# Row preparations due at the second place behind their turning, and k's turning behind its combining, in the second input stage of a transformer block

## The chip, the cores and the metric

The kernel runs on one core of a Trainium2 chip. Its engines work in parallel, each through its own queue in order: TensorE (PE, matrix products; PEld is its weight load), VectorE (DVE), ScalarE (ACT), GpSimd (POOL) and SyncE (SP, which here only starts DMA transfers). GpSimd and ScalarE start DMA transfers too. On-chip data lie in SBUF, and PE writes its sums to PSUM, eight banks of 128 partitions by 512 float32 numbers. The metric is the device time of one execution in microseconds (us).

## The reference

One block of a diffusion transformer with conditioning, in float32: batch B = 2, N = 2048 tokens, C = 576 features, H = 16 heads of 36, and an MLP of width 2304.

```python
mod = silu(c) @ w_ada + b_ada
sh_msa, sc_msa, g_msa, sh_mlp, sc_mlp, g_mlp = split(mod, 6)
xn = ln(x, 1e-6) * (1 + sc_msa) + sh_msa
q, k, v = split_heads(xn @ w_qkv + b_qkv)
q = ln(q, 1e-5, qn_g, qn_b); k = ln(k, 1e-5, kn_g, kn_b)
attn = softmax(q @ k.T * hd**-0.5)
x = x + g_msa * (attn @ v @ w_proj + b_proj)
xn2 = ln(x, 1e-6) * (1 + sc_mlp) + sh_mlp
x = x + g_mlp * (gelu(xn2 @ w1 + b1) @ w2 + b2)
```

What matters here is the third and fourth step for the second batch element: the products that give q, k and v, the norm of q and k over the 36 numbers of each head, and how their rows reach the layout in which the attention reads them.

## The kernel before

The program goes through these stages: the inputs of batch element 0 (`inputs` with b = 0), its attention (`attend`), its output projection (`outputs`), then the same three for element 1, and the MLP for both. The change touches only the input stage of element 1, `in_pairs` inside `inputs`, and of the later stages only the start of the second attention lies near it.

**Pairs of token tiles.** The 2048 tokens are 16 tiles of 128 (NT = 16). Tiles 0 and 1 are done one by one; then a loop takes pairs t0 = 2, 4, ..., 14. For each pair and for each of k (w = 1), q (w = 0) and v (w = 2), in this order, `seven_products` computes the 2 x 2 block product with seven block products instead of eight (sums of the inputs and of the weights are formed beforehand). PE writes them in four groups, (1), (2, 6), (5, 7) and (4, 3), each into one tile `s` of two PSUM banks. There are four such tiles, so group i of the next product needs the tile that group i of this one has filled.

**Combining.** `combined` gives the work that empties these tiles: ScalarE copies product 1 (`copied`), and five DVE steps, `do[0]` to `do[4]` (lines 1253 to 1257), make the outputs. `do[0]` reads (2, 6), `do[1]` reads (5, 7), `do[2]` product 4, `do[3]` product 5 and `do[4]` product 3. So (2, 6) is free behind `do[0]`, (5, 7) behind `do[3]`, (4, 3) behind `do[4]`. The prediction counts these as steps 1 to 5.

**Finishing.** `finishing` returns five pieces for k or q of a pair: the square on ScalarE (`ks`, `qs`), the sum over each head on DVE (`kr`, `qr`, L1296), the root on ScalarE (`kq`, `qq`), the reciprocal on DVE with the scaling on GpSimd (`kd`, `qd`, L1303 and L1305), and the turning, `turned_out` (`kt`, `qt`): DVE transposes 32 x 32 squares (L1309), and eight DMA transfers store the rows by feature in DRAM (L1312), seven from SP's queue and one from GpSimd's.

**Row preparations.** The attention reads keys and queries by feature from SBUF tiles `km`, `ke` (keys) and `qm`, `qe` (queries of one block of 512). For the first head pair their rows are fetched within this stage, as soon as they are stored: `turned_out` calls `take_k_block` or `take_q`, which issue the loads on SP (L817 and L819) and return the DVE work that follows, the row preparations. A key block has one preparation, with four DVE instructions (L852 on `km`; L852, L861 and L862 on `ke`). The queries have two: one instruction on `qm`, and three on `qe`. These are put into the list `taken`. Key tiles 0 to 3 are taken with k of pair 2, tiles 4 to 7 with pair 6, 8 to 11 with pair 10, 12 and 13 with pair 12, 14 and 15 with pair 14; the queries of tiles 0 to 3 with q of pair 2, whose turning stands in the loop's next round.

**The order.** The queues of DVE, SP, GpSimd and ScalarE run in the order in which the program is written here, and so does PE's. `rows_made` takes one entry of `taken`, if there is one, and issues its DVE work. It is called at three places of a round: behind `do[0]` of k, behind `do[1]` of q, and behind `qd` in v's part (this last not in the last pair). Behind v's `do[1]`, the rest of v's combining and q's turning are put off to the next round, where they stand behind ScalarE's copy and ahead of k's `do[0]`. What is left in `taken` at the end of the stage, one preparation, goes to the attention.

**The next pair's tokens.** Each round issues the loads of the next pair's tokens at its start on GpSimd's queue (`features_begun`); behind `kd`, ScalarE applies scale and shift (`input_modulated`), and GpSimd forms the sums for the seven products (`token_sums`).

Of the kernel before, what the change touches and what calls it, by code (L numbers as in the profile page):

```python
# [31 lines left out]
def dit_block(  # L32
# [724 lines left out]
    def block_of_small():  # L757
# [53 lines left out]
        def rows_taken(queue, main, ends, halves, first, src, dst):  # L811

            rest = HD - DIMS
            for c in halves:
                for h in range(2):
                    r0, f0 = 32 * (2 * c + h), first + h * HD
                    queue.dma_start(out=main[r0 : r0 + DIMS, dst], in_=qk_rows["dram"][f0 : f0 + DIMS, src(c)])  # L817
                    values = qk_rows["dram"][f0 + DIMS : f0 + HD, src(c)]
                    queue.dma_start(  # L819
                        out=ends[r0 : r0 + 4 * rest, dst],  # L820
                        in_=values.unsqueeze(1).to_broadcast([rest, 4, values.shape[1]]),
                    )
# [26 lines left out]
        def scaled(dst, part, rows, w, of_ends=0):  # L849

            gain, bias = (gb_at[rows, of_ends, i, w : w + 1] for i in range(2))
            nc.vector.tensor_scalar(dst, part, gain, bias, ALU.mult, ALU.add)  # L852
# [39 lines left out]
        def take_q(p, qb):  # L892
            i, full = qb % 2, slice(0, P)
            src = lambda c: slice(qb * BLK, (qb + 1) * BLK)
            rows_taken(nc.sync, qm[i], qe[i], range(2), p * 2 * HD, src, slice(0, BLK))
            return [lambda: scaled(qm[i], qm[i], full, 0), lambda: parted(qe[i], full, 0)]
# [190 lines left out]
        def inputs(b, weights, making, work, xnts, turned, loaded):  # L1087

            wq, wq4, bq = weights
            both, squares, taken = {}, {}, []  # L1090
# [166 lines left out]
                    lambda: tt(dst(0, 1), dst(0, 1), single(out[3]), ALU.add),  # L1257
                ], lambda: nc.scalar.copy(one, out[1])

            pairs = {}  # L1260

            def token_sums(t0):

# [9 lines left out]
            def features_begun(t):  # L1273
                if t < NT and t not in xnts:
                    xnts[t] = input_loaded(turned.pop(t), nc.gpsimd, work if t % 4 == 3 else None)

            def pair_opened(w, t0):
                pairs[w] = work.tile([P, 2, C], F32, name="pair", bufs=4)
                both.update({(w, t0 + t): pairs[w][:, t, :] for t in range(2)})

            def flat(w):
                return pairs[w].rearrange("p t f -> p (t f)")

            def finishing(w, t0):

                pair = flat(w)
                n = 2 * H
                held_ = {}

                def squares_made():  # L1290
                    held_["sq"] = work.tile([P, 2 * C], F32, name="sq", bufs=1)
                    nc.scalar.activation(held_["sq"], pair, AF.Square)

                def summed_up():
                    var = held_["var"] = work.tile([P, n], F32, name="var", bufs=2)
                    nc.vector.tensor_reduce(var, held_["sq"].rearrange("p (h d) -> p h d", d=HD), AX.X, ALU.add)  # L1296

                def rooted():
                    nc.scalar.activation(held_["var"], held_["var"], AF.Sqrt, bias=eps5, scale=1.0 / HD)

                def divided():
                    inv = work.tile([P, n], F32, name="inv", bufs=2)
                    nc.vector.reciprocal(inv, held_["var"])  # L1303
                    heads = pair.rearrange("p (h d) -> p h d", d=HD)
                    nc.gpsimd.tensor_tensor(heads, heads, inv.unsqueeze(2).to_broadcast([P, n, HD]), ALU.mult)  # L1305

                def turned_out():
                    turned_qk = work.tile([P, 2 * C], F32, name="turned_qk", bufs=2)
                    nc.vector.transpose(turned_qk, pair)  # L1309
                    for t in range(2):  # L1310
                        for g in range(P // SQ):
                            (nc.gpsimd if 2 * t + g == 5 else nc.sync).dma_start(  # L1312
                                out=by_square[t0 + t, g][:, w * NSQ : (w + 1) * NSQ, :],
                                in_=turned_qk[g * SQ : (g + 1) * SQ, t * C : (t + 1) * C].rearrange(
                                    "p (k j) -> p k j", j=SQ
                                ),
                            )
                    if w == 1:
                        if t0 % 4 == 2 and t0 < NT - 2:
                            taken.append(take_k_block(t0 - 2, t0 + 2))  # L1320
                        elif t0 >= NT - 4:
                            taken.append(take_k_block(t0, t0 + 2))
                    elif t0 == TPB - 2:
                        taken.extend(take_q(0, 0))

                return squares_made, summed_up, rooted, divided, turned_out

            def rows_made():
                if taken:
                    taken.pop(0)()  # L1330

            def in_pairs():

                sums = work.tile([P, 4, 2, 3, HALF], F32, name="weight_sums")
                less = work.tile([P, 3, HALF], F32R, name="wq4_less")
                nc.sync.dma_start(out=less.bitcast(F32), in_=saved["less"])
                for w in (1, 0, 2):
                    nc.sync.dma_start(out=sums[:, :, :, w, :], in_=saved["sums"][:, :, :, w, :])
                spread, ones = bias_rows()

                for w in (1, 0):
                    pair_opened(w, 0)
                features_begun(3)
                k = product(1, 0)
                biased(1, k, 0)
                q = product(0, 0)
                biased(0, q, 0)
                v = product(2, 0)
                biased(2, v, 0)
                k = product(1, 1)  # L1350
                biased(1, k, 1)
                input_modulated(b, xnts[3])
                more = token_sums(2)
                ks, kr, kq, kd, kt = finishing(1, 0)
                ks(), kr(), kq(), kd()
                q = product(0, 1)
                biased(0, q, 1)
                qs, qr, qq, qd, qt = finishing(0, 0)
                qs(), qr(), qq()
                kt()  # L1360
                qd()
                v = product(2, 1)
                biased(2, v, 1)
                rest = [qt]

                for t0 in range(2, NT, 2):
                    last = t0 == NT - 2
                    operands = sums, less, spread, ones, more
                    for t in range(2):
                        features_begun(t0 + 2 + t)  # L1370

                    pair_opened(1, t0)
                    do, copied = combined(1, t0, seven_products(1, t0, operands))
                    copied()
                    for step in rest:
                        step()
                    do[0]()
                    rows_made()
                    do[1]()
                    do[2](), do[3](), do[4]()  # L1380
                    ks, kr, kq, kd, kt = finishing(1, t0)
                    ks()

                    pair_opened(0, t0)
                    do, copied = combined(0, t0, seven_products(0, t0, operands))
                    copied()
                    kr(), kq()
                    do[0]()
                    kd()
                    if not last:  # L1390
                        for t in range(2):
                            input_modulated(b, xnts[t0 + 2 + t])
                        more = token_sums(t0 + 2)
                    do[1]()
                    rows_made()
                    kt()
                    do[2](), do[3](), do[4]()
                    qs, qr, qq, qd, qt = finishing(0, t0)
                    qs()

                    do, copied = combined(2, t0, seven_products(2, t0, operands))
                    copied()
                    qr(), qq()
                    do[0]()
                    qd()
                    if not last:
                        rows_made()
                    do[1]()
                    if not last:
                        rest = [*do[2:], qt]  # L1410
                        continue
                    do[2](), do[3](), do[4]()
                    qt()
                    return taken
# [89 lines left out]
            taken = key_rows[-2:]  # L1504
# [711 lines left out]
```

## Time and profile before

| | us |
|---|---|
| median of three runs | 3165.39 (3161.59 to 3166.11) |
| the profiled execution, as timed | 3166.04 |
| its span in the profile | 3164.7 |
| second input stage, first pair product to first score of the attention | 1111.85 to 1318.82 |
| attention behind it and the rest | 1318.82 to 3164.70 |

The profile is of one execution. A time such as 1141.03 counts from the span's start. In a row of a timeline stand the start, the duration, the engine, the source line, the operation, output and inputs by name, their shapes and the count; in brackets how long the engine had been idle before and what it waited for. In the view of waits, a row names who waited, for whom, how long in total, how many times, and the longest. In the table of windows, a row gives a stretch of time and its length, the busy time of each engine in it, the mean clock granted to PE (1.00 is full), the share in which the DMA engines were busy and GB/s.

### The profile page before, as it was taken

To read this page: it belongs to the slowest core of one execution; us is meant where nothing else is said; L and a number is where in the kernel's file an instruction comes from. 1 tells how busy PE (TensorE), PEld (TensorE's weight loads), DVE (VectorE), ACT (ScalarE), POOL (GpSimd) and SP (SyncE) were. 2 spreads that over 40 slices of the span, in tenths; PEclk is the share of its full clock that TensorE was granted. 3 is DMA by queue.
4 is the path that set the end of the run, shared out by engine and by line. 5 is a ranking of instruction groups with operands and counts; after the bars stand their busy time and mean duration, and the time that the engine had idled before them with its cause. 6 is when DMAs were issued, how large, how long until landed. Compare 5 with 4: busy or idle time off the path is not lost. (4 is left out here: it accounts for less than half of the span.)

```text
span 3164.7 us, 46996 instructions
## 1 busy us (share of the span) xinstructions
PE 3112.9 (98%) x17511; PEld 1856.2 (59%) x17511; DVE 1566.2 (49%) x2287; ACT 1477.3 (47%) x2853; POOL 713.5 (23%) x1005
## 2 busy tenths in 40 slices
PE   8999999999999988999999999999999999999999
PEld 5883333333334767633333333358888888777777
DVE  6773444444444555434443444345566554545454
ACT  2336666766666023366666666633565552000000
POOL 4550110123321444200011111012333320111121
PEclk9999999999999999999999999999999999999999
DMA  5773332233341743411122222145544444333331
GB/s 146 185 144 86 104 88 57 74 95 90 95 112 52 232 78 70 87 43 34 46 59 71 77 64 69 56 153 189 163 133 136 132 116 159 111 120 116 117 105 39
DMA packets 294838, 324.65 MB, mean 103 GB/s; under 512 B 168904, under 2 KB 225160, under 8 KB 292488
## 3 DMA queue, kind: packets, MB, share of 16 engines
q1 hardware_dynamic: 246464, 198.32, 21.8%
q0 software_dynamic: 46960, 117.92, 14.3%
q10 hardware_dynamic: 1176, 5.31, 0.5%
q8 instruction: 141, 2.31, 0.3%
q14 instruction: 97, 0.79, 0.1%
HBM read 200.50 MB, written 110.43 MB: 98 GB/s over the span
## 5 line engine op out<-in xcount | busy, mean ns | idle before, releaser
L1531 ACT ACTIVATE pt<-b 128x512 f32<-128x512 f32 x2048 | 1057.5, 610 | 482.9 <-PE b L1540 267.3
L1540 PE MATMUL b<-pt,vt 128*64 128x512 f32 x4096 | 935.0, 598 | 2.1 <-ACT pt L1531 2.1
L1540 PEld LDWEIGHTS b<-pt,vt 128*64 128x64 f32 x4096 | 271.8, 136 | 584.3 <-issue 437.7
L1527 PE MATMUL b<-qm,km 32*128 32x512 f32 x4096 | 563.8, 613 | 0.0
L1592 DVE TENSOR_TENSOR ot<-b,ot 128x512 f32<-128x512 f32 x192 | 132.8, 692 | 589.0 <-PE b L1540 589.0
L1527 PE MATMUL b<-qe,ke 16*128 16x512 f32 x2048 | 420.2, 791 | 0.0
L2128 PE MATMUL s<-ws,as 128*128 128x288 f32 x1440 | 351.8, 406 | 0.0
L1527 PEld LDWEIGHTS b<-qm,km 32*128 32x128 f32 x4096 | 190.6, 184 | 271.2 <-ACT pt L1531 211.1
L2128 PEld LDWEIGHTS s<-ws,as 128*128 128x128 f32 x1440 | 273.6, 190 | 75.6
L1143 PE MATMUL s<-wq,xnt 128*128 128x288 f32 x864 | 226.9, 406 | 2.6 <-ACT xnt L400 2.1
L1559 DVE RECIPROCAL den<-den 128x512 f32<-128x512 f32 x64 | 213.6, 3337 | 11.7 <-DMA den<-den_dram 11.7
L1968 PE MATMUL m<-xnt,wb 128*128 128x256 f32 x864 | 210.6, 379 | 2.7 <-DVE cs L2002 1.8
L1968 PE MATMUL m<-s,wb 128*128 128x256 f32 x864 | 210.0, 379 | 0.0
L1590 DVE COPY ot<-b 128x512 f32<-128x512 f32 x64 | 44.3, 692 | 275.0 <-PE b L1540 275.0
L1143 PEld LDWEIGHTS s<-wq,xnt 128*128 128x128 f32 x864 | 157.8, 190 | 38.3 <-ACT xnt L400 1.6
L1968 PEld LDWEIGHTS m<-s,wb 128*128 128x128 f32 x864 | 164.2, 190 | 22.3
L1527 PEld LDWEIGHTS b<-qe,ke 16*128 16x128 f32 x2048 | 106.7, 184 | 114.0 <-issue 113.3
L1968 PEld LDWEIGHTS m<-xnt,wb 128*128 128x128 f32 x864 | 158.8, 190 | 22.7 <-DVE cs L2002 2.4
L2006 ACT ACTIVATE cs<-cs,b_sb 128x512 f32<-128x512 f32 x144 | 98.9, 719 | 113.9 <-DVE cs L2001 90.2
L1047 POOL DMA_DIRECT2D turned<-squares x160 | 107.5, 679 | 196.1 <-DVE squares L1042 188.5
L1064 ACT ACTIVATE xnt<-xnt,mod 128x128 f32<-128x128 f32 x244 | 100.4, 481 | 102.0 <-DMA weight_sums<-sums_kept 51.5
L2128 PE MATMUL s<-ws,hidden 128*128 128x288 f32 x576 | 142.3, 406 | 0.0
(257 smaller groups left out, 3293.3 us busy)
## 6 DMA issues: line engine op xcount, KB each, us to landing
gelu<-cs SPq DMA_DIRECT2D x144, 256.0 KB
hidden<-gelu SPq DMA_DIRECT2D x16, 2304.0 KB
spare<-in_x_dram POOLq DMA_DIRECT2D x64, 288.0 KB, 3.2
x_dram<-spare POOLq DMA_DIRECT2D x64, 288.0 KB, 2.5
qm<-qk SPq DMA_DIRECT2D x256, 64.0 KB
den<-den_dram SPq DMA_DIRECT2D x128, 128.0 KB
xnt<-turned POOLq DMA_DIRECT2D x56, 256.0 KB, 4.0
turned<-squares POOLq DMA_DIRECT2D x160, 72.0 KB, 2.6
```

The lines of the kernel that those rows point to most:

```text
L1047: queue.dma_start(out=by_square[g], in_=squares[g * SQ : (g + 1) * SQ, :].rearrange("p (k j) -> p k j", j=SQ))
L1064: nc.scalar.activation(part, part, AF.Identity, **affine(which, k, b))
L1143: nc.tensor.matmul(out_a, full[:, k, :], wq[:, k, f], start=k == 0, stop=False)
L1527: nc.tensor.matmul(ps, k[r, keys], q[r, :], start=first, stop=not first)
L1531: nc.scalar.activation(pt[:, h, :], banks[2 * c + h], AF.Exp, scale=SCALE)
L1540: nc.tensor.matmul(acc[64 * h : 64 * h + 64, :], vt[:, v0 : v0 + 64], pt[:, h, :], start=pt is pts[0][0], stop=pt is pts[-1][0],)
L1559: nc.vector.reciprocal(den, den)
L1590: nc.vector.tensor_copy(ot, acc)
L1592: nc.vector.tensor_tensor(ot, acc, ot, ALU.add)
L1968: nc.tensor.matmul(out_m[m], wb[:, slot[m], k, f * P : (f + 1) * P], moving[m](k), start=k == 0 and m in (1, 2, 5, 6), stop=k == 1 and m == 1,
L2006: nc.scalar.activation(part, part, AF.Gelu, bias=b1_sb[:, g : g + 1])
L2128: nc.tensor.matmul(ms[m], stationary[m][:, f, :], ws[m][:, f, :], start=(f == 0), stop=(f == HF - 1))
```

## The change

The list `taken` gets a second list beside it, `slots["due"]`, with one number for each entry, and a counter `slots["now"]` that `rows_made` raises by one at each call. An entry is due two calls behind its turning, and `rows_made` does nothing while the first entry isn't due. The call of `rows_made` behind k's `do[0]` is taken out, so that a round has two places: behind `do[1]` of q, and behind `qd` in v's part.

k's turning, `kt`, stood between q's `do[1]` and `do[2]`. It now stands behind q's `do[4]`, except in the last pair (t0 = 14), where it stays, and where `rows_made` is called behind `do[4]` instead. The loads of the key rows are issued in `kt`, so they move with it.

```diff
-            pairs = {}
+            pairs, slots = {}, {"now": 0, "due": []}
...
+                    before = len(taken)
                     if w == 1:
                         if t0 % 4 == 2 and t0 < NT - 2:
                             taken.append(take_k_block(t0 - 2, t0 + 2))
...
                     elif t0 == TPB - 2:
                         taken.extend(take_q(0, 0))
+                    slots["due"] += [slots["now"] + 2] * (len(taken) - before)
...
             def rows_made():
-                if taken:
+                slots["now"] += 1
+                if taken and slots["due"][0] <= slots["now"]:
+                    slots["due"].pop(0)
                     taken.pop(0)()
...
                     do[0]()
-                    rows_made()
                     do[1]()
                     do[2](), do[3](), do[4]()
                     ks, kr, kq, kd, kt = finishing(1, t0)
...
                     do[1]()
-                    rows_made()
-                    kt()
+                    if last:
+                        kt()
+                    else:
+                        rows_made()
                     do[2](), do[3](), do[4]()
+                    if last:
+                        rows_made()
+                    else:
+                        kt()
                     qs, qr, qq, qd, qt = finishing(0, t0)
                     qs()
```

## The prediction

> **What bounds the kernel now.** First I read the page's head, with the span of the profiled execution, and the row that gives TensorE's (PE's) busy tenths in forty slices of 79.1 us. Nearly all are 9, so only time in which PE stands still, or runs slowly, can be won. Two slices in the middle, 1107.6 to 1265.9 us, are 8: the second input stage.
>
> ```profile
> span 3164.7 us, 46996 instructions
> PE   8999999999999988999999999999999999999999
> ```
>
> Next the view of waits, narrowed to 1100 to 1330 us. Its columns are who waited, for whom, us in total, times, longest.
>
> ```profile
> DVE km L852 <- DMA km<-qk: 27.7, 5, 7.6
> PE s L1229 <- DVE vt L1256: 19.1, 4, 6.1
> PE s L1229 <- DVE pair L1256: 5.1, 1, 5.1
> ```
>
> PE waits five times, 24.2 us together, and each time for L1256, the fourth of the five combining steps, which is what frees the bank of products 5 and 7. VectorE (DVE) in turn waits for rows that come back from DRAM, `km` (keys) five times, the fifth behind the stage's last product, and `qm` (queries) once (its row stands further down), at L852, the first instruction of a row preparation. The timeline of DVE in the pair t0 = 2 ties the two together (start, duration; in brackets idle time before and its cause; the last row is PE's):
>
> ```profile
> 1127.28 1.38 DVE L1309 STREAM_TRANSPOSE turned_qk<-pair 128x1152 f32<-128x1152 f32 x1 [0.71 <-POOL pair L1305]
> ...
> 1141.03 0.54 DVE L852 TENSOR_SCALAR km<-km,gb_at 64x512 f32<-64x512 f32 x1 [7.61 <-DMA km<-qk]
> 1141.95 0.54 DVE L852 TENSOR_SCALAR ended<-ke,gb_at 64x512 f32<-64x512 f32 x1 [0.38 <-DMA ke<-qk]
> ...
> 1145.04 0.45 DVE L1256 TENSOR_TENSOR vt<-vt,s 128x288 f32<-128x288 f32 x1
> ...
> 1145.78 1.37 DVE L1309 STREAM_TRANSPOSE turned_qk<-pair 128x1152 f32<-128x1152 f32 x1
> ...
> 1138.54 1.13 PE L1229 MATMUL s<-weight_sums,more 128*128 128x288 f32 x4
> 1145.64 2.26 PE L1229 MATMUL s<-weight_sums,more 128*128 128x288 f32 x4 [5.97 <-DVE vt L1256]
> ```
>
> k is turned at 1127.28 and its rows are stored and loaded back. The preparation stands so soon behind, at 1133.4, that DVE stands still 7.61 + 0.38 us; v's combining is queued behind it, and PE, already in the next product, stops at its third group for 5.97 us.
>
> The price of a stop is more than the wait: behind it four matmul records take 2.26 us where they took 1.13. So I priced each stop by the window from one product's start to the next (columns: window, length, busy PE, PEld, DVE, ACT, POOL, granted clock, DMA share, GB/s). The fourth row is a product without a stop, the last but one all 21, and the last what follows the stage.
>
> ```profile
> 1136.20:1152.29 16.09, 10.12 (x41) 7.73 (x40) 6.17 (x10) 0.40 (x1) 3.76 (x7) 0.79 0.44 90
> 1152.29:1168.39 16.10, 11.01 (x40) 8.40 (x39) 7.30 (x12) 6.10 (x15) 2.71 (x2) 0.79 0.08 25
> 1200.86:1216.55 15.69, 10.64 (x40) 8.12 (x39) 6.93 (x11) 0.40 (x1) 3.75 (x7) 0.78 0.44 92
> 1240.91:1249.02 8.11, 8.11 (x41) 6.63 (x40) 5.10 (x8) 5.38 (x13) 2.54 (x2) 1.00 0.03 5
> 1257.14:1274.23 17.09, 10.99 (x41) 8.38 (x40) 7.06 (x11) 0.40 (x1) 3.99 (x7) 0.80 0.45 87
> 1290.46:1302.50 12.04, 10.02 (x40) 7.69 (x39) 6.39 (x11) 0.40 (x1) 0.70 (x1) 0.86 0.35 52
> 1111.85:1318.82 206.97, 182.75 (x800) 146.53 (x798) 107.94 (x167) 56.60 (x122) 85.97 (x102) 0.93 0.38 68
> 1318.82:3164.70 1845.88, 1834.65 (x10049) 1172.61 (x10048) 883.46 (x1241) 803.56 (x1513) 322.03 (x448) 1.00 0.34 101
> ```
>
> The unstopped product takes 8.12 us at clock 1.00 with PE busy throughout. The five stopped ones sum to 77.01; less 5 x 8.12 = 40.6, that is **36.4 us** lost: 7.97, 7.98, 7.57, 8.97, 3.92. Cross-check by the last row but one: 206.97 - 21 x 8.12 = 36.5. Of it 24.2 is PE idle and 12.2 the lower clock (0.78 to 0.86) behind the stops.
>
> **The change, part by part.** I number the products by pair and matrix: k2, q2, v2, k4 and so on; each starts 8.12 us after the one before if nothing stops. *Place A* is behind the first combining step of k, *B* behind the second of q, *C* behind the reciprocal in v. Before, each place takes whatever is listed; after, A is gone and an entry made at count n waits for n + 2. Going through the loop by hand: the key block 0-4, turned in q2 (count 1), moves from C of pair 2 to B of pair 4; the two query steps, listed at count 2, from A and B of pair 4 to C of pair 4 and B of pair 6; key blocks 4-8 and 8-12 from C of pairs 6 and 10 to B of pairs 8 and 12; key block 12-14 from C of pair 12 to the last pair, behind q's combining. No instruction is added or removed: five preparations move, and one transposition per pair.
>
> *The five waits.* Are the rows there by the new places? The DMA rows that bound the key loads in pair 2:
>
> ```profile
> 1132.44 0.70 POOL L1312 DMA_DIRECT2D qk<-turned_qk  x1
> 1135.96 0.32 SPq L817 DMA_DIRECT2D km<-qk  x1
> ...
> 1158.44 0.55 DVE L852 TENSOR_SCALAR qm<-qm,gb_at 128x512 f32<-128x512 f32 x1 [10.65 <-DMA qm<-qk]
> ```
>
> The key rows are ready 12.4 (`km`) and 13.3 us (`ke`) after the transposition's end at 1128.66. In the new schedule B of pair 4 is at k2's start plus four products and 6.6 us (below): 1111.85 + 32.5 + 6.6 = 1150.9. Even if the later transposition (2.4 us, below) delayed the rows in full, they are there at 1141.95 + 2.4 = 1144.4: 6.5 us to spare. Query rows: q's transposition stands behind the three last steps of v, which end some 1.4 us into the next k (8.3 + 1.3 behind v's start), and lasts 1.4, so it ends at 1136.2 + 2.8 = 1139.0. In the trace the rows came 11.3 us after its end (1145.78 + 1.37 to 1158.44), so 1150.3, or 1152.3 if SyncE (SP) is still busy 2 us with the key loads. Place C of pair 4 is at 1111.85 + 40.6 + 5.3 = 1157.7: 5.4 us to spare. Blocks 4-8 and 8-12 repeat the first case, and 12-14 has still longer. All five waits go: **-36.4 us**. Below this PE cannot come, since at 8.12 it is busy for the whole of a product, so no gain beyond it is taken.
>
> *What the preparations do at B.* They are no longer free of cost by waiting, but still DVE work, now between steps 2 and 3 to 5 of q. The first row below is step 3 of an unstopped k product (start 1232.79), the next three an unstopped q product (start 1240.91), and the last PE's row behind q4, where the second query step stood at B already:
>
> ```profile
> 1241.11 0.45 DVE L1255 TENSOR_TENSOR pair<-pair,s 128x288 f32<-128x288 f32 x1 [1.71 <-PE s L1235]
> ...
> 1246.75 0.76 DVE L1254 TENSOR_TENSOR pair<-s,pair 128x576 f32<-128x576 f32 x1 [0.77 <-PE s L1235]
> 1248.22 1.38 DVE L1309 STREAM_TRANSPOSE turned_qk<-pair 128x1152 f32<-128x1152 f32 x1 [0.71 <-POOL pair L1305]
> ...
> 1252.08 1.35 DVE L1296 TENSOR_REDUCE var<-sq 128x32 f32<-128x1152 f32 x1 [1.29 <-ACT sq L1292]
> ...
> 1170.73 2.10 PE L1229 MATMUL s<-weight_sums,more 128*128 128x288 f32 x8
> ```
>
> Step 2 ends 6.6 us into the product. Four key instructions (0.54, 0.54, 0.48, 0.74; with issue about 2.4) put step 3 at 9.0 and the end of step 4 at 9.9. PE needs that bank in the next product 2.34 + 1.04 = 3.4 us in (1138.54 against the start 1136.20), so at 8.1 + 3.4 = 11.5. Spare: 1.6 us. In the trace q4 had three preparing instructions and the transposition ahead of step 3, and the next product passed its second and third group without a stop (eight matmuls in one run from 1170.73). Bounds: 0, as there, and 3.92 at each of four places (the cheapest stop of the windows), 15.7. I take 0, since that row is the same place with like work.
>
> *k's turning behind the combining.* Steps 3 to 5 need the product's end, 8.3 us in (1241.11 against 1232.79, behind a wait for PE), and with 0.45 us each end at 9.6; the transposition then runs from 9.6 to 11.0 instead of 7.3 to 8.7, so 2.4 us later. It falls into time in which DVE waited anyway: 1.29 us ahead of L1296, for ScalarE's square. That square can start 0.3 us sooner, so L1296 stays within 0.4 us either way. Its DMAs: SP's seven stores move with it, the one store on GpSimd hardly does, because in that queue it stands behind the sums of the next tokens (issued at 1132.44 in pair 2, 12.5 us into q2). The key loads followed that store, at 1135.96. So the rows come at most 2.4 us later. Behind them in SP's queue stand q's stores, counted above. If the cover were gone, 1.4 us of DVE would still lie inside v's slack (1.72 us ahead of its step 3, next fence). Cost 0.
>
> *The last pair.* There k is turned first, as before. Block 12-14 (0.42 + 0.42 + 0.35 + 0.48, about 1.8 with issue) comes ahead of the reduction of q14.
>
> ```profile
> 1313.68 1.35 DVE L1296 TENSOR_REDUCE var<-sq 128x32 f32<-128x1152 f32 x1 [1.29 <-ACT sq L1292]
> 1318.93 0.45 DVE L1255 TENSOR_TENSOR vt<-vt,s 128x288 f32<-128x288 f32 x1 [1.72 <-PE s L1235]
> ```
>
> And what PE and SP do at the stage's end, of which the last sentence of this part speaks:
>
> ```profile
> 1318.82 1.81 PE L1527 MATMUL b<-qm,km 32*128 32x512 f32 x7
> 1320.13 0.30 SPq L817 DMA_DIRECT2D km<-qk  x1
> ```
>
> Of the 1.8, 1.3 fill the idle time and 0.5 is late, which the 1.72 us wait ahead of v14's step 3 takes up. Cost 0. Its wait might grow if it also waited for the loads of block 14-16, which are now issued ahead of it into the same tile; but PE's first scores read `km` from 1318.82 while a load of `km` was issued only at 1320.13, so parts of that tile are waited for separately.
>
> [...] Rows first: in the last stopped product PE was idle 2.02 us (12.04 less 10.02 busy), the clock averaged 0.86 and the stop cost 3.92. [...]
>
> **Sum.** Profiled execution 3166.04 (span 3164.7 and 1.3 around it) - 36.4 = 3129.6. The median of the three runs, 3165.39, lies 0.65 lower: **3129.0 us** (1.15% less).
>
> **The rivals.** (1) *The preparation at B comes too late for the bank* at four places (q4, q6, q8, q12): up to 15.7 given back, 3129 to 3145, by the middle 3137. For it: only 1.6 us spare, and GpSimd works beside it. Against it: q4's row. 10%. (2) *One load is still late*, most likely the queries', with one stop of about 8 left: 3137. For it: SP's queue holds eight loads behind seven stores. Against: 5.4 us to spare. 6%. (3) *The change doesn't do what it says*, the waits being set by something that moves along, or the attention behind takes the time back: 3165. Against: PE is 1834.65 us busy of the 1845.88 that follow the stage, so nothing there was waiting for slack. 3%. (4) *Slower*: SP holds the loads so long that DVE stands at the new places longer than at the old. The place B lies 20 us behind the transposition's end; a stop cost as much as DVE's wait (7.97 for 7.61 + 0.38), so the mean old loss of 7.3 is back when rows come 27.3 us after that end, against 12.4 to 13.3 seen. At 30 us each stop would cost 10, five 50, so 3165.4 + 50 - 36.4 = 3179. 3%.
>
> **Chances and range.** Forecast 78%, and the rivals as given. The runs before scatter from 3161.6 to 3166.1, so the forecast itself holds about 3125 to 3132; up to 3141 takes in most of rivals 1 and 2. Range 3125 to 3141. Some 0.2% (6 us) is what a measurement of this kernel tells from no change. Faster: forecast, 1 and 2, with some of 3: 0.95; within: 0.02; slower: 0.03.
>
> **What would show it.** Right: all product windows 8.12 at clock 1.00, the stage from k2 to the first score near 170.5 us; no wait of `km` or `qm` L852 for DMA before the attention; L1309 of k about 9.6 us into q; L1305 and the sums on GpSimd as now. Wrong: PE idle at L1229 with L1256 as releaser in v4, v6, v8 or v12 (rival 1), or with L852 waiting for DMA ahead of it (2, 4); or an unchanged stage. A first product of a pair waiting for GpSimd's sums would be a new stop that I have priced at nothing.

## The result, and the profile after

The changed kernel takes 3129.09 us (median of four runs, 3128.95 to 3130.70), the kernel before, in the same comparison, 3163.49 us (3159.86 to 3166.11). The ratio is 0.9893, with a 95% interval of 0.9876 to 0.9910. The forecast was 3129.0.

The page's head of the changed kernel: the span, and PE's busy tenths in forty slices, which are 78.2 us each now.

```profile
span 3127.3 us, 47006 instructions
...
PE   8999999999999999999999999999999999999999
```

The two slices with an 8 in the middle are gone. The table of windows, in the columns that the prediction explained: three single products (k4, q4 and k8, in each of which PE had stood still for 5 to 6 us before), then the stage, then all that follows.

```profile
1136.20:1144.31 8.11, 8.11 (x40) 6.64 (x39) 4.08 (x6) 0.40 (x1) 3.60 (x6) 1.00 0.78 164
1144.31:1152.42 8.11, 8.11 (x40) 6.63 (x39) 5.81 (x9) 5.37 (x13) 2.72 (x2) 1.00 0.33 72
1184.89:1193.01 8.12, 8.12 (x41) 6.65 (x40) 4.08 (x6) 0.40 (x1) 4.05 (x7) 1.00 0.83 179
...
1111.85:1282.37 170.52, 170.52 (x801) 139.38 (x799) 109.99 (x167) 56.60 (x122) 87.22 (x102) 1.00 0.46 83
1282.37:3127.30 1844.93, 1834.74 (x10049) 1172.60 (x10048) 883.29 (x1241) 803.66 (x1513) 319.16 (x448) 1.00 0.33 101
```

The stage takes 170.52 us, all of it with PE busy at clock 1.00. It took 206.97, so 36.45 us went there. What follows got 0.95 shorter, 1844.93 for 1845.88, without any part of the change in it. A second profile of the kernel before (`before_again`) has 3165.0 - 1319.72 = 1845.3 there, and one of the changed kernel (`after_again`) 3126.5 - 1282.03 = 1844.5, so a part of this difference is scatter, and I read nothing into the rest.

In the view of waits, narrowed to 1100 to 1290 us, no row of PE for L1256 is left, and one row of L852 for DMA, which lies behind the stage:

```profile
DVE km L852 <- DMA km<-qk: 3.7, 1, 3.7
```

The timeline of DVE in q4 shows a key block in its new place (q4 starts at 1144.31), and below it GpSimd beside it:

```profile
1150.16 0.76 DVE L1254 TENSOR_TENSOR pair<-s,pair 128x576 f32<-128x576 f32 x1 [0.77 <-PE s L1235]
1150.83 1.04 DVE L852 TENSOR_SCALAR km<-km,gb_at 64x512 f32<-64x512 f32 x1
1151.80 0.67 DVE L852 TENSOR_SCALAR ended<-ke,gb_at 64x512 f32<-64x512 f32 x1
1152.51 0.48 DVE L861 TENSOR_SCALAR high<-ended,part 64x512 fp32r<-64x512 f32 x1
1153.02 0.74 DVE L862 SCALAR_TENSOR_TENSOR ke<-ended,part,high 64x512 fp32r<-64x512 f32 x1
...
1154.16 0.45 DVE L1256 TENSOR_TENSOR pair<-pair,s 128x288 f32<-128x288 f32 x1
...
1154.90 1.37 DVE L1309 STREAM_TRANSPOSE turned_qk<-pair 128x1152 f32<-128x1152 f32 x1
1156.27 1.35 DVE L1296 TENSOR_REDUCE var<-sq 128x32 f32<-128x1152 f32 x1
```

```profile
1149.47 2.12 POOL L1305 TENSOR_TENSOR pair<-pair,inv 128x1152 f32<-128x1152 f32 x1 [9.22 <-DVE inv L1303]
1151.56 0.63 POOL L395 TENSOR_TENSOR xnt<-tail,xnt 128x128 fp32r<-128x128 f32 x1
```

No idle time stands ahead of L852 or behind it. Step 4 (L1256) ends at 1154.61, 10.3 us into q4, the transposition stands behind the combining, and L1296 follows it at once, so the 1.29 us in which DVE used to wait there are filled.

The loads of that block on SP's queue:

```profile
1137.49 0.32 SPq L817 DMA_DIRECT2D km<-qk  x1
```

They begin 1.5 us later than before (1135.96), since the transposition and SP's stores come later, and 13 us ahead of the preparation.

### The profile page after: what moved, and what is told of

Same layout as the page of the kernel before. It is cut to its first block, busy times and chain, and to the rows that moved or that the text cites. A ratio compares the mean times of both kernels' runs of the same rounds, so it can differ in the third digit from the quotient of the medians.

```text
span 3127.3 us, 47006 instructions
## 1 busy us (share of the span) xinstructions
PE 3100.6 (99%) x17511; PEld 1849.1 (59%) x17511; DVE 1568.5 (50%) x2287; ACT 1477.3 (47%) x2853; POOL 712.6 (23%) x1005
## 3 DMA queue, kind: packets, MB, share of 16 engines
q0 software_dynamic: 46960, 117.92, 14.5%
```

## The experiments

The theory: the 36.4 us are the five waits of DVE for rows just stored, with PE's slower clock behind each, and the due numbers take them away; the moved turning only keeps the bank of products 5 and 7 in time. The rivals: the moved turning, or the dropped place A, is what counts; the spare time at B is by luck just enough; the price of a stop is not what the windows of before said. A `held_up` in a diff stands for `nc.vector.reciprocal` on so many columns of data that are there anyway, written to a scratch tile. The times before in each line are those of the kernel before in the same comparison.

### The due numbers alone

```diff
                     do[1]()
-                    if last:
-                        kt()
-                    else:
-                        rows_made()
+                    rows_made()
+                    kt()
                     do[2](), do[3](), do[4]()
-                    if last:
-                        rows_made()
-                    else:
-                        kt()
```

> Only the due numbers and the dropped place A; k's turning stays ahead of q's steps 3 to 5, and the last pair has no exception. Theory (the gain is that the five preparations no longer wait for their loads; the moved turning only keeps the bank of products 5 and 7 in time): all five stops go. At B four key instructions (2.9 us with the wait for GpSimd seen in the changed kernel) and the transposition (1.4) now both lie ahead of step 3, so step 4 ends about 11.7 us into q, against 11.5 at which PE needs the bank: stops of 0.2 to 0.4 us in v4, v8 and v12, none in v6, so 3129 to 3132. Rival 1 (the moved turning carries part of the gain itself): 3135 or more. Rival 2 (without it each of the four places stops PE at the price of the cheapest old stop, 3.92): about 3143.

And the changed kernel again beside it:

> The changed kernel as it is, as the measure for its neighbours: 3129, stage from k2 to the first score 170.5 us, no stop of PE in it.

Measured: 3129.54 us for the due numbers alone (ratio to before 0.9891, 0.9875 to 0.9908) and 3128.60 for the changed kernel (0.9890, 0.9874 to 0.9907). The times don't tell them apart. The windows do: of 21 products, three are longer than 8.12, just v4, v8 and v12.

```profile
1152.75:1161.23 8.48, 8.36 (x40) 6.56 (x39) 7.02 (x12) 2.79 (x6) 5.00 (x7) 1.00 0.49 71
1201.80:1210.29 8.49, 8.36 (x41) 6.57 (x39) 6.61 (x11) 2.79 (x6) 5.01 (x7) 1.00 0.51 71
1250.86:1259.48 8.62, 8.35 (x40) 6.56 (x39) 6.72 (x11) 2.79 (x6) 5.01 (x7) 1.00 0.51 72
```

They lose 0.36, 0.37 and 0.50, together 1.2 us, with the clock at 1.00. So the due numbers bring the gain, and the moved turning takes three small stops away behind key blocks. Both rivals fall, the one that priced a place at 3.92 too.

### The turning alone

```diff
                     do[1]()
                     rows_made()
-                    kt()
+                    if last:
+                        kt()
                     do[2](), do[3](), do[4]()
+                    if not last:
+                        kt()
```

> Only k's turning moved; rows_made at its three places and as soon as possible, as before. Theory: the five waits stay, and those at C grow by the 1.5 us by which the key loads were issued later in the changed kernel (1137.49 against 1135.96 in pair 2): four stops longer by 0 to 1.5 us, so 3163 to 3170. Rival (the moved turning frees PE by itself): below 3160.

Measured: 3172.93 us against 3161.57, ratio 1.0029 (1.0019 to 1.0040): slower than before, and 3 us above the range that I had expected. The five stops stand where they were. The products last 15.96 (k4), 16.03 (q4), 18.31 (k8), 17.81 (k12) and 14.91 (k14), a loss of 42.4 us instead of 36.4, which fits the span of this profile (3171.1 against 3164.7). The medians lie further apart than the spans, since the execution of the kernel before that was profiled (3166.04) was one of its longer ones. The waits say where it is from:

```profile
DVE km L852 <- DMA km<-qk: 35.7, 5, 9.4
...
PE s L1229 <- DVE vt L1256: 24.3, 4, 7.0
```

The wait for `km` grew from 27.7 to 35.7 us, because the stores, and so the loads, come later while the preparations stay. k4 and q4 didn't get longer and k8 and k14 by 2.6 and 2.9, so 1.5 us for each was not the measure of it. The rival falls: the turning moved by itself frees nothing and costs 6 us in the stage.

### Due at the first place instead of the second

```diff
-                    slots["due"] += [slots["now"] + 2] * (len(taken) - before)
+                    slots["due"] += [slots["now"] + 1] * (len(taken) - before)
```

> As the changed kernel, but due at the first place behind the turning instead of the second. Theory: the four key blocks of pairs 2, 6, 10 and 12 are prepared at C of their own pair again, so the stops in k4, k8, k12, k14 come back with 7.97 + 7.57 + 8.97 + 3.92 = 28.4, and up to 1.5 more each for the later loads; the queries at B and C of pair 4 come late enough not to wait, since k4 has been stopped. So 3157.5 to 3163.5, and no stop in q4. Rival (place A or the turning's place is what counts, not the distance): 3129 to 3137.

Measured: 3175.72 us against 3161.57, ratio 1.0041 (1.0026 to 1.0055). Four stops came back, as the theory said, in k4, k8, k12 and k14 (17.92, 17.92, 17.27 and 14.49 us, a loss of 35.1), and q4 has none. But the time is 12 us above the forecast. PE's view of waits from 1290 to 1340 us, and then DVE's and PE's timelines, show a stop that I had not counted:

```profile
PE b L1536 <- DVE vt L1253: 10.3, 1, 10.3
```

```profile
1308.62 1.38 DVE L1309 STREAM_TRANSPOSE turned_qk<-pair 128x1152 f32<-128x1152 f32 x1 [0.71 <-POOL pair L1305]
...
1324.57 0.42 DVE L852 TENSOR_SCALAR km<-km,gb_at 64x256 f32<-64x256 f32 x1 [13.38 <-DMA km<-qk]
```

Block 14-16, listed at count 12 in the last pair, is due at count 13, right behind its own loads. DVE waits 13.38 us for them, v14's combining stands behind it, and the attention's first scores have no bank. So that step of my expectation was wrong: I had followed four key blocks, and there are five.

### The same, with the last block left to the attention

```diff
                     do[2](), do[3](), do[4]()
-                    if last:
-                        rows_made()
-                    else:
+                    if not last:
                         kt()
```

> As due_one, but the last pair prepares nothing, so block 14-16 goes to the attention as in the changed kernel. Theory (due_one came out 12 to 18 us over its forecast because block 14-16, listed at count 12, was due at count 13 in the last pair, right behind its own loads; DVE stood 13.4 us there and the attention's first scores waited 10.3 us for v's bank): the stop at the attention's start goes and the four stops of due_one stay, 9.8 + 9.8 + 9.2 + 6.4 = 35.1, so 3129 + 35 = 3164, and no wait of a first score for DVE. Rival (the rest of due_one's excess lies elsewhere): 3170 or more.

Measured: 3164.05 us against 3162.39, ratio 1.0003 (0.9994 to 1.0013). The four stops stay (17.92, 17.55, 17.45, 14.31, a loss of 34.8), and PE's only wait in the stretch from 1105 to 1340 us is

```profile
PE s L1229 <- DVE vt L1256: 24.9, 4, 7.1
```

So the excess of the run before was that one stop, 11.7 us by the medians of the two kernels and 14.5 between the spans of their profiles (3177.5 and 3163.0). And the distance is what counts, not the dropped place: with A gone and the turning moved, but the rows due one place earlier, nothing of the gain is left.

### Due at the third place

```diff
-                    slots["due"] += [slots["now"] + 2] * (len(taken) - before)
+                    slots["due"] += [slots["now"] + 3] * (len(taken) - before)
```

> As the changed kernel, but due at the third place. Theory: the rows have landed by the second place, so a later one brings nothing more, and the preparations at C find no less spare time than at B: 3129 within 0.1%. Block 12-14 goes to the attention as well, where it is wanted with the third group. Rival (some wait hidden so far was still there at the second place): below 3127. Rival (two preparations in the attention's first blocks come too late): over 3132.

Measured: 3130.41 us against 3163.06, ratio 0.9895 (0.9879 to 0.9912), the stage 170.53 us. The second place is late enough; a third brings nothing that these runs can tell. The profile has 0.5 us of PE's waiting at the attention's start that the changed kernel hasn't:

```profile
1284.83 0.66 PE L1536 MATMUL b<-qm,km 32*128 32x512 f32 x1 [0.54 <-PE b L1536]
```

### Without the exception for the last pair

```diff
                     do[1]()
-                    if last:
-                        kt()
-                    else:
-                        rows_made()
+                    rows_made()
                     do[2](), do[3](), do[4]()
-                    if last:
-                        rows_made()
-                    else:
-                        kt()
+                    kt()
```

> The changed kernel without its exception for the last pair: block 12-14 is prepared at B and k turned behind q's combining there too. Theory: k's stores and the loads of block 14-16 come up to 2.4 us later, but the attention needs that block only with its third or fourth group of keys, over 10 us behind its start, so within 0.1% of 3129. Rival (the end of the stage waits for that block): 3130 to 3133.

Measured: 3129.47 us against 3163.06, ratio 0.9891 (0.9875 to 0.9908), the stage 170.52 us. The exception makes no difference that these runs can tell.

### More work at B

```diff
                     else:
                         rows_made()
+                    held_up(sums, {2: 512, 4: 128, 8: 288, 10: 640, 12: 480}.get(t0, 0))
                     do[2](), do[3](), do[4]()
```

> The changed kernel with DVE work added at B, between q's steps 2 and 3, to find where the bank of products 5 and 7 comes too late: reciprocals of 512 columns in pair 2 (3.3 us, no preparation there), 128 in pair 4 (0.8, with a key block), 288 in pair 8 (1.9, key block), 640 in pair 10 (4.2, none) and 480 in pair 12 (3.1, key block). In the changed kernel step 4 ended 9.3 us into q without a preparation and 10.3 with a key block. Theory (needed at 11.5): no stop in v2 (10.8) and v4 (11.2), 0.7 us in v8, 0.4 in v10, 2.0 in v12; with the lower clock behind them about twice that, so 3135. Rival (the spare time is smaller, as a place for the preparation that just happened to fit): stops in v2 and v4 too, 3138 or more. Rival (spare time is larger than thought): 3129 to 3131.

Measured: 3133.15 us against 3163.06, ratio 0.9908 (0.9892 to 0.9925), the stage 174.30 us. The stops are those of the theory: none in v2 and v4, and in v8, v10 and v12

```profile
1205.31 1.21 PE L1229 MATMUL s<-weight_sums,more 128*128 128x288 f32 x4 [0.80 <-DVE pair L1256]
...
1230.11 1.21 PE L1229 MATMUL s<-weight_sums,more 128*128 128x288 f32 x4 [0.21 <-DVE pair L1256]
...
1256.72 1.21 PE L1229 MATMUL s<-weight_sums,more 128*128 128x288 f32 x4 [2.03 <-DVE pair L1256]
```

The step that frees the bank, in q4, without a stop behind it, and in q8:

```profile
1154.98 0.45 DVE L1256 TENSOR_TENSOR pair<-pair,s 128x288 f32<-128x288 f32 x1
```

```profile
1204.71 0.46 DVE L1256 TENSOR_TENSOR pair<-pair,s 128x288 f32<-128x288 f32 x1
```

In q8 (start 1192.91) step 4 ends at 12.26 and PE stood 0.80, so the limit is 11.46 us; in q4 (start 1144.2) it ends at 11.2 and nothing stands still. The 11.5 of the prediction is confirmed. The stops cost 1.04, 0.46 and 2.26 us, little more than they last, where my expectation had doubled them.

### Stops without a DMA

```diff
                     if not last:
                         rows_made()
+                    held_up(sums, {2: 768, 6: 896, 8: 1024, 10: 1280, 12: 1536}.get(t0, 0))
                     do[1]()
```

> The changed kernel with DVE work added at C of pairs 2, 6, 8, 10 and 12: reciprocals of 768, 896, 1024, 1280 and 1536 columns, by 3337 ns for 512 columns 5.0, 5.8, 6.7, 8.3 and 10.0 us (an estimate). It makes stops of PE in the next k without any DMA in them. Step 4 of v ends 5.3 + x + 1.9 us into v, PE needs the bank at 11.5, so PE is idle about 0.7, 1.5, 2.4, 4.0 and 5.7 us, 14.3 in all. Theory by the old rows (a stop of 2.02 us cost 3.92, one of 5 to 6 cost 7.6 to 9): about 1.4, 3, 4.6, 6.5 and 8.5, so 3153, with the clock below 1.00 behind each. [...]

Measured: 3151.41 us against 3163.06, ratio 0.9962 (0.9948 to 0.9977), with stops made of nothing but DVE work. The windows of k4, k8, k10, k12 and k14:

```profile
1136.16:1144.80 8.64, 8.35 (x40) 6.55 (x39) 6.49 (x9) 0.40 (x1) 3.60 (x6) 1.00 0.60 139
1185.38:1195.36 9.98, 8.34 (x40) 6.55 (x39) 7.84 (x9) 0.40 (x1) 4.05 (x7) 1.00 0.61 134
1211.60:1222.89 11.29, 8.35 (x40) 6.56 (x39) 9.15 (x9) 0.40 (x1) 4.57 (x8) 1.00 0.50 104
1239.12:1252.81 13.69, 10.01 (x40) 7.67 (x39) 9.85 (x10) 0.40 (x1) 4.02 (x7) 0.88 0.54 112
1269.05:1286.48 17.43, 10.96 (x40) 8.35 (x39) 12.65 (x10) 0.40 (x1) 1.07 (x2) 0.80 0.34 53
```

PE was idle 0.29, 1.64, 2.94, 3.68 and 6.47 us. The first three lost 0.52, 1.86 and 3.17, idle time and 0.23 more, at clock 1.00; the last two 5.57 and 9.31, at 0.88 and 0.80. The profile is of the shortest of five executions (3149.65). The other four took 1.0 to 1.9 us more at a mean clock of 0.997 instead of 0.998, which would fit one more stop with a lower clock behind it; no profile shows it. So a held-up DVE is enough to make the old stops, price and all, and here the three short stops cost some 0.23 us more than they lasted, and not the 1.4, 3 and 4.6 us that the old rows gave. That left one question: why did the old stop of 2.02 us in k14 have the slower clock behind it?

### Six short stops, six middle ones, and the kernel before again

Both edits stand at the same place as that of the run above.

```diff
+                    held_up(sums, {2: 944, 4: 944, 6: 928, 8: 928, 10: 928, 12: 928}.get(t0, 0))
```

> As stops_made, with about 2.0 us of PE idle in each of k4, k6, k8, k10, k12 and k14 (928 or 944 columns at C of the pair before; by 1.64 for 896 and 2.94 for 1024). It asks whether the stop of 2.02 us in k14 of the kernel before, behind which the clock was 0.51 for 3 us, is the rule for that length. [...] Theory B (it depends on where the gap falls, so that some of six show the lower clock): one to four with 1.5 to 2 us more each, 3145 to 3150. Theory C (the old row is the rule): 3.9 each, 3152.

```diff
+                    held_up(sums, {2: 1056, 4: 1056, 6: 1040, 8: 1040, 10: 1040, 12: 1040}.get(t0, 0))
```

> The same with about 3.1 us of idle in each of the six (1040 or 1056 columns). [...] Theory B: more of them with the lower clock than in short_stops, 3151 to 3161. Theory C: all of them with it, about 5.2 each, 3160.

> The kernel before, profiled a second time: 3162, stops of the same five places; does the short one in k14 (2.02 us idle) have the lower clock behind it again? [...]

Measured, one run each: 3148.58, 3151.59 and 3166.41 us. The windows of k4 to k14 with the short stops, and three of the middle ones (k4, k8, k10):

```profile
1136.38:1146.12 9.74, 8.36 (x40) 6.56 (x39) 7.60 (x9) 0.40 (x1) 3.59 (x6) 1.00 0.57 126
1162.35:1176.54 14.19, 11.34 (x40) 8.56 (x39) 9.06 (x9) 0.40 (x1) 4.70 (x8) 0.76 0.51 101
1192.77:1202.95 10.18, 8.35 (x40) 6.55 (x39) 8.04 (x9) 0.40 (x1) 4.04 (x7) 1.00 0.56 126
1219.18:1231.53 12.35, 10.01 (x40) 7.71 (x39) 8.55 (x9) 0.40 (x1) 4.56 (x8) 0.86 0.59 115
1247.77:1257.41 9.64, 8.36 (x40) 6.56 (x39) 7.49 (x9) 0.40 (x1) 4.00 (x7) 1.00 0.62 135
1273.63:1286.13 12.50, 10.02 (x40) 7.74 (x39) 8.70 (x9) 0.40 (x1) 1.07 (x2) 0.86 0.45 70
```

```profile
1134.41:1146.69 12.28, 10.01 (x40) 7.74 (x39) 8.45 (x10) 0.40 (x1) 3.59 (x6) 0.86 0.58 121
...
1193.77:1204.83 11.06, 8.36 (x40) 6.56 (x39) 8.88 (x10) 0.40 (x1) 4.03 (x7) 1.00 0.55 121
1221.06:1232.63 11.57, 8.35 (x40) 6.56 (x39) 9.39 (x10) 0.40 (x1) 4.54 (x8) 1.00 0.51 103
```

All stops of PE in this stage, by their idle time in the timelines of these runs:

| PE idle, us | stops | clock 1.00 behind it | lower clock behind it |
|---|---|---|---|
| 0.2 to 1.9 | 8 | 8 | none |
| 2.0 to 3.4 | 12 | 2.03, 2.17, 2.70, 2.94, 3.22 | 2.02, 2.11, 2.27, 2.34, 2.48, 2.85, 3.36 |
| 3.6 to 7.5 | 24 | none | 24 |

The first kind lost its idle time and some 0.25 us, the last 1.8 to 3.2 us more than it lasted, and the middle kind the one or the other: 3.17 for 2.94 us, and 6.07 for 2.85. So theory B holds: between 2 and 3.4 us the length alone doesn't decide. Its further guess, more lower clocks with the middle stops than with the short ones, doesn't: each run has three of six, and the stops came out as 1.28 to 2.85 us and 2.17 to 3.73 us, not as equal as planned. In the kernel before, k14 came out alike in both profiles (2.02 and 2.11 us idle, both with the lower clock).

What decides can be read from the traces, which record every change of the granted clock. In each execution that has any, the falls and returns of this stage lie whole multiples of 3.413 us apart, to within 0.003 us, and they don't follow the stops: in the profile of the kernel before it fell at 1142.41, 1159.47, 1207.26, 1265.29 and 1296.01, and came back 6.83 us later, the last time 3.41. I divided the stage by this grid in all 14 profiles. Behind the 31 pieces of 3.413 us in which PE was idle for 2.01 us or more the clock fell to 0.50, and behind the other 708 with a full clock, most of them without any idle time and none with more than 1.98 us, it stayed at 1.00. Two stops of the second run that fall across two pieces each show the edge, 3.22 us with 1.97 of it in the first piece, and 3.36 us with 2.02:

```profile
1223.09:1226.50 3.41, 1.44 (x7) 0.84 (x5) 3.38 (x3) 0.00 (x0) 1.81 (x3) 1.00 0.54 173
1226.50:1229.91 3.41, 2.16 (x10) 1.77 (x11) 3.26 (x6) 0.00 (x0) 0.36 (x1) 1.00 0.00 0
1277.70:1281.11 3.41, 1.39 (x7) 0.82 (x5) 3.38 (x3) 0.00 (x0) 0.00 (x0) 1.00 0.11 32
1281.11:1284.52 3.41, 2.07 (x5) 1.53 (x6) 3.27 (x6) 0.00 (x0) 0.27 (x1) 0.50 0.02 5
```

The clock came back at the end of the first low piece that had at most 0.23 us of idle (31 times), and not behind one with 0.73 or more (24 times). By these rows I estimate the price: the idle time, half of the time for which PE works at the lower clock (four matmuls took 2.26 us there and 1.13 at the full one), and some 0.2 us. The old stop in k14 lay in one piece as a whole, so the next one was slow throughout: 2.02 + 3.41 / 2 + 0.2 = 3.9, for 3.92 measured. The limit of 2.0 us is one of this stage, by the ends of the matmuls as the trace models them; for matmuls of other shapes it is not shown.

## Why the prediction was right, and where it was off

**The sum.** The five stops went, all of them and nothing else: 36.45 us in the stage for 36.4 forecast, the stage 170.52 for 170.5. That each stop's price was read from its own window, with the slower clock in it, made the sum right; the idle time alone would have given 24.2. The last step of the sum is luck: the 0.65 us were taken off because the median of three lay lower than the profiled run, which is no reason for the changed kernel to be faster, and what happened to stand against it is the part behind the stage, 0.95 us shorter without any part of the change in it. The medians of the two kernels lie 34.4 us apart and not 36.4, since the kernel before scatters (3159.86 to 3166.11) and its profile is of a long execution. Three runs stand behind the cause: the due numbers alone bring it, the turning alone doesn't, and rows due one place earlier lose all of it.

**The places.** Rows were ready ahead of B and C in every pair, as worked out. The key loads came 1.5 us later, within the 2.4 allowed for. The run with a third place shows that no wait was left hidden at the second.

**The preparation at B.** This term was mis-sized, without an effect on the sum. I put it at 2.4 us, with step 4 ending at 9.9 us and 1.6 to spare. It took 2.9, ended at 10.3, and left 1.2, mostly because the first instruction lasted 1.04 us instead of 0.54. The limit of 11.5 was right (11.46 in the run with more work at B). The prediction gave the moved turning a cost of 0 and looked for no gain in it. With the longer preparation its old place would have been over the limit: that is the 1.2 us of the run with the due numbers alone, and all that the moved turning is worth here.

**The last pair.** No wait, no gain: without the exception the time is the same.

**The clock's price for short stops.** Here a step of the prediction failed, in the price of rival 1: by one row, 3.92 us lost for 2.02 idle, it set 15.7 us for four short stops. Twenty stops of up to 3.4 us show that below 2 us none has that price, and above it seven of twelve. The three small stops that the due numbers alone left cost 0.4 each. What the runs show in its place is that a short stop pays for the clock only if some 2.0 us of it fall into one piece of the grid of 3.413 us: behind seven gaps of 2.02 to 3.36 us the clock was lower, and behind five of 2.03 to 3.22 us it stayed at 1.00. Had the last old stop been one of the second kind, it would have cost some 2.3 us and the sum would have been 34.8, an estimate from the short stops, which lost 0.25 us more than they lasted.

**The slower rival.** Its mechanism is real, rows that land after their place: the turning alone lengthened the stops by 6 us, and the last block, due right behind its loads, cost 11.7 by the medians. It needed rows later or places earlier than in the changed kernel.

## What to carry to other kernels

An instruction that waited for a load held up all that stood behind it on its engine: with rows due at the first place, DVE's wait of 13.38 us in the last pair kept the attention's first scores waiting for 10.3. Where the load is a round trip through DRAM, give its consumer a due time counted from the issue, in places of the engine's own order, and put the issue no later than it must be. Price a stop of PE by the stretch from one unit of work to the next, not by the idle time, and don't carry the price of one short stop over to others: whether the clock fell behind it depended here on where it lay, and 2.94 us of idle cost 3.17 and 2.85 cost 6.07. Before moving work between the release of two banks, work out by when the next product needs the bank: here 1.2 us of spare time decided between no stop and three small ones.

## What the runs showed of the hardware that had not been expected

The first key instruction at B took 0.93 to 1.04 us instead of 0.54 in q4, q8 and q12, where GpSimd's scaling (L1305) was under way: in q4 that ran from 1149.47 to 1151.59, and L852 from 1150.83 to 1151.87. So its end came 0.28 us behind GpSimd's; in the last pair, where GpSimd's scaling was over, the same instruction on half the columns took 0.42 us, as before. The 14 profiles of this stage have 42 rows of L852 that began while L1305 was under way. The 40 on 512 columns all ended 0.28 or 0.29 us behind the end of L1305, whether that made them 0.66 or 2.35 us long, and the two on 256 columns ended 0.15 us behind it. The longest stand in the run with the third place, below with GpSimd's row:

```profile
1158.57 2.34 DVE L852 TENSOR_SCALAR ended<-ke,gb_at 64x512 f32<-64x512 f32 x1
```

```profile
1158.37 2.26 POOL L1305 TENSOR_TENSOR pair<-pair,inv 128x1152 f32<-128x1152 f32 x1
```

So where the two overlapped, the end of L852 went by that of L1305; why, no run here shows.

Gaps of 2.0 to 3.4 us on PE left its clock alone or halved it for 3.4 or 6.8 us. What decided was how much of the gap fell into one piece of the grid of 3.413 us on which the changes of the clock lie: 1.98 us did not halve it in this stage, 2.01 us did.
